# Two attention layers on one core: sums in the full array shape turned as whole tiles and added by DVE; layer-1 reciprocals spread one turn later, beside the maxima

## The chip, the cores and the metric

The kernel runs on one core of a Trainium2 chip. The metric is the time of one execution on the device, in microseconds (us). The engines are TensorE (PE in the profile; PEld is its weight load), VectorE (DVE), ScalarE (ACT), GpSimd (POOL) and SyncE (SP, which here only issues DMAs). All data are 32-bit floats.

## The reference

Two attention layers over images of 4 x 128 channels x 4096 positions (64 x 64). For each of the 4 images:

```
layer 0:  g, theta, phi = 1x1 projections of x to 64 channels
          f = theta^T phi                      (4096 x 4096)
          x = W (softmax(f) g) + b + x         (128 channels again)
layer 1:  q, k, v = 1x1 projections of x, 128 channels
          x = x + softmax(q^T k / sqrt(128)) v
```

The softmax runs over the 4096 keys of each query. For it a kernel needs, per query, the largest score, the exponentials of the scores less that maximum, and their sum.

## The kernel before, in words

The work is cut into 64 chunks, each of 512 queries of one image and one layer: 8 chunks per image and layer. The first 8 are layer 0 of image 0. Then layer-0 chunks of the next image alternate with layer-1 chunks of this one (chunks 8 to 55), and the last 8 are layer 1 of image 3. The list is `chunks`; chunk g is its g-th entry.

A chunk's keys are taken in 16 pieces p of 256 (two halves of 128, the partitions of a tile). Score tiles therefore have keys on partitions and the 512 queries along the free dimension, 128 x 2 x 512. The program is one long hand-written order: `slot(t)` writes the instructions of slot t, 16 slots to a turn, and the instructions of each engine run in the order in which the slots write them. In turn T the scores of chunk T are made; the later steps of the earlier chunks run beside them:

- `scores` (slot t, PE, lines 187 and 246) writes a score tile `ps` in PSUM. There are two of these tiles, so the scores of slot p wait until those of slot p-2 have been read.
- `copy` (ACT, L253) copies ps to SBUF as `s`; `maxima` (DVE, L260 and L262) takes the running maximum `mx` of ps. The maximum of a slot is the last reader of its ps.
- At the next turn's start `max_merge` (DVE, L265) folds the two halves of mx; at slot 1 `max_turn` (PE, L270) turns mx by four transposes into `pt`, `max_columns` (DVE, L275) takes the maximum along the free dimension, and `max_spread` (PE, L282) spreads it again over all partitions by four more transposes, as `o_mx`.
- `subtract` (DVE, L290) 18 slots after the scores, `exps` (ACT, L294) after 19, `sums` (POOL, L306, L308 and L311) right behind them: POOL adds the 16 exponential tiles of a chunk into `sum`, 128 partitions x 512 queries in the end. `values` (PE, lines 343 to 356) multiplies with the values 20 and 21 slots after the scores and gathers `acc` (and in one mode `hi`) in PSUM.
- `leave` (ACT L360, DVE L362) moves acc to SBUF as `y`, at slot 4, two turns after the scores.

What is left of a chunk is done by `finish()` in three steps, at slots that `out_slots(g)` gives:

- `sum_columns` and `invert`: sum still has one partial sum per partition. Matmuls with a column of ones as the moving operand add over the partitions, 128 queries at a time, into `pc` (128 x 4, queries on partitions, PE, L187); DVE takes the reciprocal `rc` (L373).
- `sum_spread` and `normalize`: four transposes spread rc over all partitions as `o_rc` (PE, L282), and DVE multiplies y by it (L381).
- `project_out` and `residual`: in layer 0 the projection W (PE, `po`), then y or po, the bias and x are added on DVE (L393 in layer 0, L396 in layer 1). In layer 1 the result goes out by DMA (L397), and the next x tile is loaded (L90).

`pt`, `pc`, `o_rc`, `po` and the query projection `pq` all use the one PSUM tile of the pool `ps_m`; each has to be read before the next is written.

The array of PE is used in three shapes. `mode(t)` names the one of a pair of slots by what runs in them: "row" (scores of layer 0 beside values of layer 1; 64 rows, two matmuls at once), "col" (layer 0 on either side; 64 columns, two at once), and "full" (layer 1 on both sides). `cut` splits a matmul into two halves of 64 columns in col mode. The transposes always use the whole array.

In the alternating stage a layer-1 chunk's three steps come at slots 7, 9 and 11 of the second turn after its own, which scores a layer-1 chunk too. Those of a layer-0 chunk would fall into a row-mode turn there and come at slots 1, 3 and 5 of the turn after, again one that scores a layer-1 chunk. So before the change all three steps of both kinds lie in turns with layer-1 scores. At slots above 5, `finish()` follows the maxima of the slot; at slots up to 5 it follows the values, and `max_spread` if there is one.

Of the kernel before, what the change touches and what calls it, by code (L numbers as in the profile page):

```python
# [10 lines left out]
F32 = mybir.dt.float32  # L11
AF = mybir.ActivationFunctionType
ALU = mybir.AluOpType
AX = mybir.AxisListType
# [3 lines left out]
def kernel(  # L18
# [39 lines left out]
    nc = tc.nc  # L58
    B, C, N = x.shape
    IC = thT.shape[1]  # L60
    P = 128
    NB = 512
    NCH = N // NB
    KT = NB // P
    NPR = N // (2 * P)
# [10 lines left out]
    w2 = ctx.enter_context(tc.tile_pool(name="w2", bufs=2))  # L76
# [4 lines left out]
    ps_m = ctx.enter_context(tc.tile_pool(name="ps_m", bufs=1, space=bass.MemoryType.PSUM))  # L81

    def const(name, shape):
        return cp.tile(shape, F32, tag=name, name=name)
# [10 lines left out]
    ident = const("ident", [P, P])  # L95
# [64 lines left out]
    chunks = [(0, 0, c) for c in range(NCH)]  # L160
# [5 lines left out]
    NG = len(chunks)  # L166
    begin = {ch: BT * g for g, ch in enumerate(chunks)}

    def layer_at(t, lag):
        g = (t - lag) // NPR  # L170
        return chunks[g][0] if 0 <= g < NG else None

    def mode(t):

        t -= t % 2
        ls, lv = layer_at(t, 0), layer_at(t, VL)
        if ls == 0 and lv == 1:
            return "row"
        return "col" if lv == 0 or ls == 0 else "full"

    now = ["full"]

    def cut(out, lhsT, rhs, start=True, stop=True):

        cols = [slice(0, IC), slice(IC, P)] if now[0] == "col" else [slice(0, P)]
        for c in cols:
            nc.tensor.matmul(out[c], lhsT=lhsT[:, c], rhs=rhs, start=start, stop=stop)  # L187
# [8 lines left out]
    SUM = {}  # L196
# [31 lines left out]
    def proj_q(g):  # L228
        layer, b, c = chunks[g]
        pq = ps_m.tile([P, NB], F32, tag="m", name=f"pq_{g}")  # L230
        cut(pq, weights[layer][0], X[b, c])
        q = w3.tile([P, NB], F32, tag="q", name=f"q_{g}")
        nc.scalar.activation(q, pq, AF.Identity, bias=weights[layer][1])
        Q[g] = q
# [29 lines left out]
    def max_merge(g):  # L264
        nc.vector.tensor_tensor(M[g][:, 0, :], M[g][:, 0, :], M[g][:, 1, :], ALU.max)  # L265

    def max_turn(g):
        pt = ps_m.tile([P, KT, P], F32, tag="m", name=f"pt_{g}")
        for i in range(KT):
            nc.tensor.transpose(pt[:, i, :], M[g][:, 0, ts(i, P)], ident)  # L270
        M[g] = pt

    def max_columns(g):
        mc = w2.tile([P, KT], F32, tag="mc", name=f"mc_{g}")
        nc.vector.reduce_max(mc, M[g], AX.X)  # L275
        M[g] = mc
# [8 lines left out]
    def max_spread(g):  # L285
        BC[g] = spread(ps_b, "b", f"mx_{g}", M.pop(g))
# [71 lines left out]
    def leave(g):  # L358
        y = w2.tile([P, NB], F32, tag="y", name=f"y_{g}")
        nc.scalar.copy(y, ACC.pop(g))  # L360
        if g in HI:
            nc.vector.tensor_tensor(y, HI.pop(g)[0], y, ALU.add)  # L362
        ACC[g] = y

    def sum_columns(g):
        pc = ps_m.tile([P, KT], F32, tag="m", name=f"pc_{g}")
        for i in range(KT):
            cut(pc[:, i : i + 1], SUM[g][:, 0, ts(i, P)], ones[:, 0:1])
        SUM[g] = pc

    def invert(g):
        rc = w2.tile([P, KT], F32, tag="rc", name=f"rc_{g}")
        nc.vector.reciprocal(rc, SUM[g])  # L373
        SUM[g] = rc

    def sum_spread(g):
        SUM[g] = spread(ps_m, "m", f"rc_{g}", SUM[g])

    def normalize(g):
        y = ACC[g]  # L380
        nc.vector.tensor_tensor(y, y, SUM.pop(g), ALU.mult)  # L381

    def project_out(g):
        if chunks[g][0] == 0:
            po = ps_m.tile([P, NB], F32, tag="m", name=f"po_{g}")
            cut(po, wo0, ACC[g])
            ACC[g] = po

    def residual(g):
        layer, b, c = chunks[g]  # L390
        if layer == 0:
            t = X[b, c]
            nc.vector.scalar_tensor_tensor(t, ACC.pop(g), bo0, t, ALU.add, ALU.add)  # L393
        else:
            t = X.pop((b, c))
            nc.vector.scalar_tensor_tensor(t, ACC.pop(g), bv1, t, ALU.add, ALU.add)  # L396
            nc.sync.dma_start(out=out[b, :, ts(c, NB)], in_=t)  # L397
            if loads:
                load(*loads.pop(0))

    def out_slots(g):

        t = (g + 2) * NPR
        if chunks[g][0] == 0 and mode(t + 8) == "row":
            return [t + NPR + q for q in (1, 3, 5)]
        return [t + q for q in (7, 9, 11)]

    def query_slot(g):
        t = (g - 1) * NPR + 13
        return t if mode(t) != "row" else (g - 2) * NPR + 15  # L410

    queries = {query_slot(g): g for g in range(1, NG)}
    cols, spreads, outs = ({out_slots(g)[k]: g for g in range(NG)} for k in range(3))

# [2 lines left out]
    def at(table, batch, *job):  # L419
        table.setdefault(batch, []).append(job)  # L420

    at(later, BT, small_products, 0, 0)
    for b in range(B):
        at0, at1 = begin[0, b, 0], begin[1, b, 0]
        for j in range(NCH):
            if b == 0:
                if j:
                    at(mid, j - 1, keys0, b, j)
                at(later, BT + 1 + j, values0, b, j)
            elif b == 1:  # L430
                at(mid, at0 - 7 + j, keys0, b, j)
                at(later, at0 + 2 + j, values0, b, j)
            else:
                at(mid if j < NCH - 2 else later, at0 - 6 + j, keys0, b, j)
                at(later, at0 - 6 + j, values0, b, j)
            ready = out_slots(chunks.index((0, b, j)))[2] // 2 + 1
            at(later, max(ready, at1 - (7 if b == B - 1 else 9) + j), keys1, b, j)
            at(later, max(ready, at1 + 2 + j), values1, b, j)

    def of(t, lag):  # L440

        g, p = divmod(t - lag, NPR)
        return (g, p) if 0 <= g < NG else None

    def run(fn, gp):
        if gp is not None:
            fn(*gp)

    def slot(t):
        turn, p = divmod(t, NPR)  # L450
        m = turn - 1 if 0 <= turn - 1 < NG else None
        now[0] = mode(t)
        f = turn - 2 if 0 <= turn - 2 < NG else None
        if p == 0 and m is not None:
            max_merge(m)
        if p == 4 and f is not None:
            leave(f)
        run(scores, of(t, 0))
        run(copy, of(t, 0))
        run(exps, of(t, EL))  # L460
        run(sums, of(t, EL))
        run(subtract, of(t, SL))
        if p == 1 and m is not None:
            max_turn(m)
            max_columns(m)
        run(maxima, of(t, 0))
        run(own_sums, of(t, EL + 1))

        def finish():
            if t in cols:  # L470
                sum_columns(cols[t])
                invert(cols[t])
            if t in spreads:
                sum_spread(spreads[t])
                normalize(spreads[t])
            if t in outs:
                project_out(outs[t])
                residual(outs[t])
            if t in queries:
                proj_q(queries[t])  # L480

        if p > 5:
            finish()
        if p % 2 == 0:
            for fn, b, j in mid.get(t // 2, []):
                fn(b, j)
        else:
            run(values, of(t, VL + 1))
            run(values, of(t, VL))
            if p == 1 and m is not None:  # L490
                max_spread(m)
            if p <= 5:
                finish()
            for fn, b, j in later.get(t // 2, []):
                fn(b, j)
# [41 lines left out]
```

## Time and profile before

| | |
|---|---|
| median of 3 runs | 3079.7 us (3072.96 to 3080.42) |
| the profiled execution | 3076.04 us |
| its span | 3074.3 us |
| granted PE clock over the span | 0.998 |
| busy: PE, DVE, POOL, ACT | 3019.3, 2532.6, 2383.8, 2096.9 us |
| pc matmuls, full shape / in 64 columns | 264 / 496 records, 31.5 / 18.4 us |
| pt, o_mx, o_rc transposes | 256 records each, 40.3, 40.1, 40.5 us |
| L275 reduction along the free dimension | x64, mean 0.684 us |
| L381 normalize / L396 residual of layer 1 | x64, mean 0.682 us / x32, mean 0.774 us |

A row of the groups or of a timeline names the line, the engine, the operation, and the tiles "out<-in" with shapes; a timeline line begins with start and duration in us, and several instructions of a kind that follow each other are merged with their count. In brackets stands the idle time of the engine just before, and what ended it. A matmul of 32-bit floats appears as two records, a transpose as one. Matmuls overlap in the pipeline, so a group's duration runs into the next group; the distance from start to start is the time that it takes from the engine.

### The profile page before, as it was taken

To read this page: it belongs to the slowest core of one execution; us is meant where nothing else is said; L and a number is where in the kernel's file an instruction comes from. 1 tells how busy PE (TensorE), PEld (TensorE's weight loads), DVE (VectorE), ACT (ScalarE), POOL (GpSimd) and SP (SyncE) were. 2 spreads that over 40 slices of the span, in tenths; PEclk is the share of its full clock that TensorE was granted. 3 is DMA by queue.
4 is the path that set the end of the run, shared out by engine and by line. 5 is a ranking of instruction groups with operands and counts; after the bars stand their busy time and mean duration, and the time that the engine had idled before them with its cause. 6 is when DMAs were issued, how large, how long until landed. Compare 5 with 4: busy or idle time off the path is not lost.

```text
span 3074.3 us, 35878 instructions
## 1 busy us (share of the span) xinstructions
PE 3019.3 (98%) x13484; PEld 1243.5 (40%) x13484; DVE 2532.6 (82%) x2337; ACT 2096.9 (68%) x2306; POOL 2383.8 (78%) x1025
## 2 busy tenths in 40 slices
PE   8999999999999999999999999999999999999998
PEld 3222343344443444433344444444333444444444
DVE  6999878888888788888888877888888886766677
ACT  6888867666667676776666776667766676555554
POOL 3999878777888677887878877788878776666667
PEclk9999999999999999999999999999999999999999
DMA  2000000000000000000000000000000000000000
GB/s 67 1 1 1 1 1 8 8 8 4 4 8 8 8 8 1 8 8 8 7 6 2 8 4 4 4 1 4 4 4 4 4 0 4 4 4 7 4 4 11
DMA packets 11534, 19.47 MB, mean 6 GB/s; under 512 B 2656, under 2 KB 3168, under 8 KB 11360
## 3 DMA queue, kind: packets, MB, share of 16 engines
q1 hardware_dynamic: 10896, 17.14, 1.7%
q8 instruction: 106, 1.74, 0.2%
q14 instruction: 68, 0.56, 0.1%
q10 hardware_dynamic: 464, 0.03, 0.0%
HBM read 8.79 MB, written 8.39 MB: 6 GB/s over the span
## 4 chain that ended last, share of the span: by engine, by line
PE 88%; DVE 6%; issue 3%; ACT 3%; POOL 1%; ACTq 0%; DVEq 0%; POOLq 0%
PE ps L187 29%; PE acc L351 15%; PE acc L356 12%; PE ps L246 11%; PE acc L343 11%; DVE mx L262 5%; PE pq L187 2%; ACT s L253 2%; PE pv L187 1%; PE pc L187 1%; PE pt L270 1%; PE o_mx L282 1%; DVE s L290 1%; PE o_rc L282 1%; PE po L187 1%
## 5 line engine op out<-in xcount | busy, mean ns | idle before, releaser
L308 POOL TENSOR_TENSOR sum<-sum,s 128x1024 f32<-128x1024 f32 x891 | 2150.6, 2414 | 494.5 <-ACT s L294 450.9
L253 ACT COPY s<-ps 128x1024 f32<-128x1024 f32 x1024 | 1032.2, 1008 | 853.7 <-PE ps L187 560.4
L262 DVE TENSOR_TENSOR mx<-ps,mx 128x1024 f32<-128x1024 f32 x896 | 1093.9, 1221 | 417.6 <-ACT s L253 417.0
L290 DVE TENSOR_TENSOR s<-s,o_mx 128x1024 f32<-128x1024 f32 x1024 | 1233.2, 1210 | 15.1 <-PE o_mx L282 13.3
L294 ACT ACTIVATE s<-s 128x1024 f32<-128x1024 f32 x1024 | 1090.0, 1065 | 16.5 <-DVE s L290 16.1
L187 PE MATMUL ps<-q,k 128*64 128x512 f32 (+1 forms) x3232 | 929.5, 594 | 2.8 <-ACT k L217 2.8
L246 PE MATMUL ps<-q,k 64*128 64x512 f32 x2048 | 519.3, 613 | 25.4 <-DVE mx L262 24.1
L187 PEld LDWEIGHTS ps<-q,k 128*64 128x64 f32 (+1 forms) x3232 | 325.5, 151 | 506.3 <-issue 445.0
L343 PE MATMUL acc<-s,v 128*64 128x512 f32 x2048 | 497.8, 601 | 8.7 <-ACT s L294 8.7
L352 PE MATMUL hi<-s,v 64*128 64x512 f32 x1104 | 496.0, 589 | 0.0
L351 PE MATMUL acc<-s,v 64*128 64x512 f32 x1104 | 496.0, 589 | 0.0
L356 PE MATMUL acc<-s,v 128*128 128x512 f32 x944 | 424.8, 593 | 0.8 <-ACT y L360 0.7
L351 PEld LDWEIGHTS acc<-s,v 64*128 64x128 f32 x1104 | 205.9, 187 | 260.7 <-issue 202.7
L246 PEld LDWEIGHTS ps<-q,k 64*128 64x128 f32 x2048 | 179.6, 186 | 299.9 <-DVE mx L262 149.1
L306 POOL TENSOR_TENSOR sum<-s,s 128x1024 f32<-128x1024 f32 x64 | 152.1, 2376 | 180.8 <-ACT s L294 180.5
L356 PEld LDWEIGHTS acc<-s,v 128*128 128x128 f32 x944 | 175.3, 190 | 203.3 <-issue 187.4
L343 PEld LDWEIGHTS acc<-s,v 128*64 128x64 f32 x2048 | 131.0, 136 | 279.7 <-issue 157.0
L352 PEld LDWEIGHTS hi<-s,v 64*128 64x128 f32 x1104 | 205.9, 187 | 0.0
L260 DVE TENSOR_TENSOR mx<-ps,s 128x1024 f32<-128x1024 f32 x64 | 78.0, 1218 | 22.5 <-ACT s L253 18.9
L265 DVE TENSOR_TENSOR mx<-mx 128x512 f32<-128x512 f32 x64 | 90.4, 1413 | 2.2
L311 POOL TENSOR_TENSOR sum<-sum 128x512 f32<-128x512 f32 x63 | 80.3, 1275 | 4.9
L187 PE MATMUL pq<-x,wq 128*64 128x512 f32 (+1 forms) x240 | 66.6, 598 | 0.0
(49 smaller groups left out, 846.0 us busy)
## 6 DMA issues: line engine op xcount, KB each, us to landing
x<-in_x_dram SPq DMA_DIRECT2D x32, 256.0 KB, 3.3
out_dram<-x SPq DMA_DIRECT2D x32, 256.0 KB, 2.0
wq<-in_theta_wT_dram SPq DMA_DIRECT2D x2, 32.0 KB, 2.9
wo<-in_W_wT_dram SPq DMA_DIRECT2D x2, 32.0 KB, 4.7
wk<-in_Wk_dram SPq DMA_DIRECT2D x1, 64.0 KB, 2.9
wv<-in_Wv_dram SPq DMA_DIRECT2D x1, 64.0 KB, 2.3
wq<-in_Wq_dram SPq DMA_DIRECT2D x1, 64.0 KB, 1.8
wk<-in_phi_wT_dram ACTq DMA_DIRECT2D x1, 32.0 KB, 3.2
```

Of the source, the lines that this page charges most:

```text
L187: nc.tensor.matmul(out[c], lhsT=lhsT[:, c], rhs=rhs, start=start, stop=stop)
L246: nc.tensor.matmul(ps[:, h, :], lhsT=K[0, b, j][rows, r, :], rhs=q[rows, :], start=True, stop=True)
L253: nc.scalar.copy(s, PS[g, p])
L262: nc.vector.tensor_tensor(M[g], ps, M[g], ALU.max)
L290: nc.vector.tensor_tensor(s, s, BC[g].unsqueeze(1).to_broadcast([P, 2, NB]), ALU.subtract)
L294: nc.scalar.activation(s, s, AF.Exp, scale=scales[chunks[g][0]])
L306: nc.gpsimd.tensor_tensor(SUM[g], S[g, 0], s, ALU.add)
L308: nc.gpsimd.tensor_tensor(SUM[g], SUM[g], s, ALU.add)
L343: nc.tensor.matmul(ACC[g][h * IC : (h + 1) * IC, :], lhsT=v, rhs=s[:, h, :], start=first, stop=last)
L351: nc.tensor.matmul(ACC[g], lhsT=v[lo], rhs=s[lo, h, :], start=first, stop=last)
L352: nc.tensor.matmul(hi, lhsT=v[up], rhs=s[up, h, :], start=(p == p0 and h == 0), stop=(p == p1 and h == 1))
L356: nc.tensor.matmul(ACC[g], lhsT=v, rhs=s[:, h, :], start=first, stop=last)
```

## The change

`sum_columns` has a second form. In full mode it turns the four 128 x 128 pieces of sum by transposes, as `max_turn` does with the maxima, into a `pc` of 128 x 4 x 128, and DVE adds along the free dimension (`reduce_sum`) into `sc`, 128 x 4 in SBUF; `invert` takes its reciprocal from there. In the other modes it is as before.

`out_slots` now gives four slots, with normalize apart from the spread. For most chunks these are the old ones. For a layer-1 chunk whose finishing turn runs in col mode, the reciprocals stay at slot 7; the spread goes to slot 1 of the next turn, where it follows `max_spread`, and normalize and residual go to slot 6 of that next turn, between the maxima of slots 6 and 7. That next turn scores a layer-0 chunk, but for the last such chunk.

```diff
--- before.py
+++ after.py
@@ -363,6 +363,15 @@
         ACC[g] = y
 
     def sum_columns(g):
+        if now[0] == "full":
+
+            pc = ps_m.tile([P, KT, P], F32, tag="m", name=f"pc_{g}")
+            for i in range(KT):
+                nc.tensor.transpose(pc[:, i, :], SUM[g][:, 0, ts(i, P)], ident)
+            sc = w2.tile([P, KT], F32, tag="sc", name=f"sc_{g}")
+            nc.vector.reduce_sum(sc, pc, AX.X)
+            SUM[g] = sc
+            return
         pc = ps_m.tile([P, KT], F32, tag="m", name=f"pc_{g}")
         for i in range(KT):
             cut(pc[:, i : i + 1], SUM[g][:, 0, ts(i, P)], ones[:, 0:1])
@@ -400,17 +409,20 @@
 
     def out_slots(g):
 
+
         t = (g + 2) * NPR
         if chunks[g][0] == 0 and mode(t + 8) == "row":
-            return [t + NPR + q for q in (1, 3, 5)]
-        return [t + q for q in (7, 9, 11)]
+            return [t + NPR + q for q in (1, 3, 3, 5)]
+        if chunks[g][0] == 1 and mode(t + 8) == "col":
+            return [t + 7, t + NPR + 1, t + NPR + 6, t + NPR + 6]
+        return [t + q for q in (7, 9, 9, 11)]
 
     def query_slot(g):
         t = (g - 1) * NPR + 13
         return t if mode(t) != "row" else (g - 2) * NPR + 15
 
     queries = {query_slot(g): g for g in range(1, NG)}
-    cols, spreads, outs = ({out_slots(g)[k]: g for g in range(NG)} for k in range(3))
+    cols, spreads, norms, outs = ({out_slots(g)[k]: g for g in range(NG)} for k in range(4))
 
 
 
@@ -433,7 +445,7 @@
             else:
                 at(mid if j < NCH - 2 else later, at0 - 6 + j, keys0, b, j)
                 at(later, at0 - 6 + j, values0, b, j)
-            ready = out_slots(chunks.index((0, b, j)))[2] // 2 + 1
+            ready = out_slots(chunks.index((0, b, j)))[3] // 2 + 1
             at(later, max(ready, at1 - (7 if b == B - 1 else 9) + j), keys1, b, j)
             at(later, max(ready, at1 + 2 + j), values1, b, j)
 
@@ -472,7 +484,8 @@
                 invert(cols[t])
             if t in spreads:
                 sum_spread(spreads[t])
-                normalize(spreads[t])
+            if t in norms:
+                normalize(norms[t])
             if t in outs:
                 project_out(outs[t])
                 residual(outs[t])
```

## Prediction

> **What bounds the kernel now.** I read the page's busy times and chain first, then the PE timeline of one steady pair of turns (a turn is the 16 slots of one chunk), then DVE and POOL in the same stretch.
>
> ```profile
> PE 3019.3 (98%) x13484; PEld 1243.5 (40%) x13484; DVE 2532.6 (82%) x2337; ACT 2096.9 (68%) x2306; POOL 2383.8 (78%) x1025
> ...
> PE 88%; DVE 6%; issue 3%; ACT 3%; POOL 1%; ACTq 0%; DVEq 0%; POOLq 0%
> ```
>
> TensorE has work nearly always and 88% of the chain is its own, so an operation taken off PE is worth its start-to-start time, except where PE waits for someone. Busy time hides where that is. A turn that scores a layer-1 chunk runs on the PE timeline from 2044.66 to 2095.62, 50.96 us; a turn that scores a layer-0 chunk from 2003.64 to 2044.66, 41.02 us. DVE's fixed work per turn (16 maxima, 16 subtractions, each starting 1.13 us after the last) is 36.2 us in both. So the layer-0 turns are where DVE is close to the bound, and the change moves work into them.
>
> The layer-1 turn on PE:
>
> ```profile
> 2048.20 0.60 PE L270 MATMUL pt<-ident,mx 128*128 128x128 f32 x4
> 2048.63 3.60 PE L356 MATMUL acc<-s,v 128*128 128x512 f32 x8
> 2052.07 0.60 PE L282 MATMUL o_mx<-ident,mc 128*128 128x128 f32 x4
> 2052.51 0.95 PE L187 MATMUL pc<-ones,sum 128*128 128x1 f32 x8
> 2053.32 3.68 PE L187 MATMUL ps<-q,k 128*128 128x512 f32 x8
> ...
> 2072.47 3.60 PE L187 MATMUL ps<-q,k 128*64 128x512 f32 x16
> 2076.01 0.65 PE L282 MATMUL o_rc<-ident,rc 128*128 128x128 f32 x4
> 2076.59 1.94 PE L343 MATMUL acc<-s,v 128*64 128x512 f32 x8
> 2078.36 3.60 PE L187 MATMUL ps<-q,k 128*64 128x512 f32 x16
> 2081.79 1.89 PE L343 MATMUL acc<-s,v 128*64 128x512 f32 x8
> 2083.51 3.60 PE L187 MATMUL ps<-q,k 128*64 128x512 f32 x16
> ```
>
> Read the distances between starts, not the durations. Four transposes take 0.43 (pt) or 0.44 (o_mx); the eight passes of pc take 0.81. The lone o_rc at slot 9 stretches its surroundings: 2072.47 to 2078.36 is 5.89, where the next pair without it, 2078.36 to 2083.51, is 5.15. It costs 0.74. No line here has an idle bracket, so PE sets this turn.
>
> The layer-0 turn, PE, then DVE and POOL:
>
> ```profile
> 2014.42 1.13 PE L246 MATMUL ps<-q,k 64*128 64x512 f32 x4 [0.43 <-DVE mx L262]
> ...
> 2023.96 1.88 PE L246 MATMUL ps<-q,k 64*128 64x512 f32 x8
> ```
>
> ```profile
> 2020.98 1.22 DVE L262 TENSOR_TENSOR mx<-ps,mx 128x1024 f32<-128x1024 f32 x1 [0.97 <-ACT s L253]
> ...
> 2022.05 4.83 POOL L308 TENSOR_TENSOR sum<-sum,s 128x1024 f32<-128x1024 f32 x2 [1.11 <-ACT s L294]
> 2022.12 1.21 DVE L290 TENSOR_TENSOR s<-s,o_mx 128x1024 f32<-128x1024 f32 x1
> ...
> 2023.25 1.22 DVE L262 TENSOR_TENSOR mx<-ps,mx 128x1024 f32<-128x1024 f32 x1
> ```
>
> These DVE lines are the maximum of slot 6, a subtraction, and the maximum of slot 7, which ends at 2024.47 and frees the score buffer that slot 9 needs. Slot 9's scores are the second half of the group at 2023.96, so they start at 2024.82. The margin is 0.35. In the three slots before, it is already gone: at 2014.42 PE waits for such a maximum.
>
> **The savings.** Sums turned in full mode: the order of the changed kernel has 33 of them: 23 at slot 1 of the layer-1 turns, 9 in the all-layer-1 stage, one in the tail. Each swaps pc (0.81) for four transposes (0.44), 0.37. On 32 of them PE is the bound: 11.8 us. The added DVE reduction is the twin of max_columns (0.68, 33 times, 22 us of DVE); it stands ahead of a subtraction in a DVE queue that waits 2.63 us for pc there, and the following maximum waits 1.63 for ACT anyway. I cost it at nothing; without that cover it would cost up to 0.68 each. The reciprocal reads 128x4 as before.
>
> The spread o_rc leaves slot 9 of 23 layer-1 turns: 23 x 0.74 = 17.0 us. Together 28.8.
>
> **The costs.** o_rc goes behind o_mx at slot 1 of the next turn, in whole-array mode already paid for: 0.44. There PE's lead is not free: the next scores start the copy, the maximum and the scores of slot 5 that wait for it, so all shifts by 0.44. 23 x 0.44 = 10.1.
>
> Normalize and residual go from slots 9 and 11 of the layer-1 turn to slot 6 of the next turn, between the maxima of slots 6 and 7. In 22 cases that is a layer-0 turn; the 23rd falls into the full stage, where the same margin is 3.87 us. What is queued behind them on DVE is a subtraction and the maximum of slot 7; PE waits for that. Two instructions by their rows: normalize 0.68; the residual waits for it, and DVE rows that wait for their predecessor (L381 then L396 in the tail) start 0.72 after it; the next starts 0.66 after a residual of 0.74. So 0.72 + 0.66 = 1.38 late.
>
> But the residual (L396) reads two SBUF tiles, y and x. What such an instruction does while POOL is adding is seen in two places:
>
> ```profile
> 3046.05 6.00 POOL L308 TENSOR_TENSOR sum<-sum,s 128x1024 f32<-128x1024 f32 x2
> ...
> 3048.10 1.72 DVE L396 SCALAR_TENSOR_TENSOR x<-y,bv,x 128x512 f32<-128x512 f32 x1
> ```
>
> ```profile
> 2134.63 4.79 POOL L308 TENSOR_TENSOR sum<-sum,s 128x1024 f32<-128x1024 f32 x2 [0.34 <-ACT s L294]
> ...
> 2137.08 2.89 DVE L265 TENSOR_TENSOR mx<-mx 128x512 f32<-128x512 f32 x1
> 2139.89 1.21 DVE L290 TENSOR_TENSOR s<-s,o_mx 128x1024 f32<-128x1024 f32 x1
> ```
>
> The first is the slowest of 32 residuals (the others take 0.74): POOL's add ended 1.17 us after it was issued, and it took that plus 0.55. The second is the merge of maxima, 0.69 in 43 turns and 2.9 in 21: there it was issued just behind the start of an add (here the second of the two, at 2137.07) and sat out its 2.35. All 30 other residuals under POOL work were issued within 0.05 us of an add's end, which is why the row looks harmless. Normalize reads one PSUM operand and takes 0.68 whatever POOL does.
>
> At its new place the residual is issued at 2020.98 + 1.14 + 0.72 = 2022.84. POOL's add started at 2022.05 (released by ACT, so tied to the same slot) and ends at 2024.42. The offset, 0.79 into the add, is the same to 0.01 in all 22 layer-0 turns. So the residual ends at 2024.42 + 0.55 = 2024.97; the subtraction starts at 2024.90, the maximum of slot 7 at 2026.03, ending 2027.25. PE's slot 9 starts 0.06 later, as at 2014.42, at 2027.31 instead of 2024.82: 2.49, and 0.10 more, since those scores took 0.96 to the next line after that stall instead of 0.86. **A new wait of 2.59 us, 22 times: 57.0 us.** The next pair absorbs the lag: DVE's maximum of slot 9 would end at 2031.78, before PE's slot 11 at 2032.56. Bounds: from below -0.35 + 0.06 + 1.38 + 0.10 = 1.19 (no wait for POOL), from above 2.59 + 2.45 (a second add goes first). I take 2.59, the reading of the 22 rows above.
>
> [...]
>
> [...]
>
> The tail: the last chunk's column sums stand alone. Transposes there take 1.22 to their reader (as o_rc at 3068.03 to 3069.25), then 0.71 for the reduction, against pc's 1.12: +0.8.
>
> **Sum.** -28.8 + 10.1 + 57.0 + 0.8 = +39.1. The profiled execution took 3076.04 (span 3074.3 and 1.7 around it), 3.7 under the median of three, 3079.7. Forecast 3115, about 1.3% slower. About 0.3%, 9 us, is what a measurement of this kernel can tell from no change.
>
> **Rivals.**
> 1. The residual doesn't sit out the add (the slow rows being something else). The wait is 1.19: 26.2 instead of 57.0, +8.3, **3084**. For it: 31 quick residuals. Against: their place at the ends of adds.
> 2. The buffer margin isn't what stops PE, because DVE makes up the lag before slot 9. Then only savings, o_rc and tail remain: -17.9, **3058**, faster. It decides once the pair's lateness stays under 0.29. Against: 2014.42 waits for exactly this release.
> [...]
>
> Chances: forecast 0.74 (own range 3102 to 3127: 0.3 us a turn and the spread of the times), rival 1 0.14, rival 2 0.06, rival 3 0.03, else 0.03. The range runs from rival 1, 3082, to 3127. Rival 1 is split around the 9 us bound. Faster 0.06, same 0.11, slower 0.83.
>
> **What would show it.** Layer-0 turns of about 44 us instead of 41.02; residual rows near 2.1 us; PE waiting some 2.5 us for the maximum at slot 9; layer-1 turns near 49.85; pc at 0.44 to its successor. Residuals at 0.74 in layer-0 turns make it rival 1; no wait at slot 9 makes it rival 2. I am wrong as well if the shorter layer-1 turn shifts POOL against DVE, or if the reduction at slot 1 delays a maximum.

## The result, and the profile after

The changed kernel takes 3147.26 us (median of 6 runs, 3144.21 to 3147.71) against 3075.99 us before (median of 6): a ratio of 1.0229, 95% interval 1.0218 to 1.0239. The forecast was 3115 us, and 3147 lies above its range, which ended at 3127. The profiled execution took 3147.71 us with a span of 3145.9, so 71.6 us more span than before.

The page of the changed kernel (the busy times and the chain, which the prediction shows for the kernel before), and its group of layer-0 scores:

```profile
PE 3035.9 (97%) x13352; PEld 1240.3 (39%) x13352; DVE 2569.9 (82%) x2370; ACT 2102.8 (67%) x2306; POOL 2386.9 (76%) x1025
...
PE 82%; DVE 10%; ACT 3%; issue 3%; POOL 2%; DMA 0%; POOLq 0%; ACTq 0%; DVEq 0%
...
L246 PE MATMUL ps<-q,k 64*128 64x512 f32 x2048 | 531.9, 622 | 75.7 <-DVE mx L262 74.5
```

PE's share of the chain falls from 88 to 82%, DVE's rises from 6 to 10. PE waits 74.5 us for maxima in front of layer-0 scores. The same group before:

```profile
L246 PE MATMUL ps<-q,k 64*128 64x512 f32 x2048 | 519.3, 613 | 25.4 <-DVE mx L262 24.1
```

PE's busy time grows by 17 us although it has 132 records fewer: its instructions themselves became slower.

The layer-1 turn after, on PE:

```profile
2108.57 0.60 PE L282 MATMUL o_mx<-ident,mc 128*128 128x128 f32 x4
2109.01 0.60 PE L370 MATMUL pc<-ident,sum 128*128 128x128 f32 x4
2109.44 3.60 PE L187 MATMUL ps<-q,k 128*128 128x512 f32 x8
```

Four transposes take 0.43 where the eight passes took 0.81. By the starts of the turns' first scores, each of the 23 layer-1 turns from turn 11 on is 1.19 us shorter (50.96 to 49.77 in a steady one).

The layer-0 turn after, first DVE, then PE:

```profile
2073.22 1.23 DVE L262 TENSOR_TENSOR mx<-ps,mx 128x1024 f32<-128x1024 f32 x1 [0.97 <-ACT s L253]
2074.36 0.68 DVE L390 TENSOR_TENSOR y<-y,o_rc 128x512 f32<-128x512 f32 x1
2075.07 2.13 DVE L405 SCALAR_TENSOR_TENSOR x<-y,bv,x 128x512 f32<-128x512 f32 x1
2077.12 1.21 DVE L290 TENSOR_TENSOR s<-s,o_mx 128x1024 f32<-128x1024 f32 x1
2078.26 1.21 DVE L262 TENSOR_TENSOR mx<-ps,mx 128x1024 f32<-128x1024 f32 x1
```

```profile
2076.20 1.02 PE L246 MATMUL ps<-q,k 64*128 64x512 f32 x4
2079.52 1.17 PE L246 MATMUL ps<-q,k 64*128 64x512 f32 x4 [2.30 <-DVE mx L262]
2080.48 1.05 PE L351 MATMUL acc<-s,v 64*128 64x512 f32 x1
...
2081.33 1.05 PE L351 MATMUL acc<-s,v 64*128 64x512 f32 x1
...
2082.19 1.05 PE L351 MATMUL acc<-s,v 64*128 64x512 f32 x1
...
2083.04 1.02 PE L351 MATMUL acc<-s,v 64*128 64x512 f32 x1
...
2083.89 0.59 PE L351 MATMUL acc<-s,v 64*128 64x512 f32 x1
...
2084.33 0.59 PE L351 MATMUL acc<-s,v 64*128 64x512 f32 x1
```

The residual takes 2.13 us; the maximum behind it is late, and PE waits 2.30 us for it at slot 9. Then comes what the prediction had not: the four matmuls after the wait start 0.85 apart, twice the usual 0.43, and take up to 1.05 us instead of 0.59. The granted clock says why. The table of stretches of the same kernel, whose columns are the stretch, its length, the busy time and instructions of PE, PEld, DVE, ACT and POOL, the granted PE clock, the DMA share and GB/s:

```profile
2077.07:2080.48 3.41, 1.11 (x6) 0.49 (x6) 3.41 (x4) 2.07 (x2) 3.27 (x2) 1.00 0.20 77
2080.48:2083.89 3.41, 3.41 (x10) 1.36 (x8) 3.41 (x4) 1.97 (x2) 2.44 (x2) 0.50 0.00 0
2083.89:2087.31 3.42, 3.42 (x18) 1.55 (x16) 1.23 (x2) 0.57 (x1) 1.38 (x1) 1.00 0.00 0
```

PE worked 1.11 of 3.41 us, and for the next 3.41 us it got half its clock. That loses half of 3.41, 1.70 us, after the wait is over. It happened in 20 of the 22 layer-0 turns with a moved residual. Those turns are 4.7 us longer than before (41.02 to 45.71); turns 24 and 40, without it, 3.0.

So the 71.6 us come to this, from the turns' starts: 23 layer-1 turns at -1.19, -27.4; 22 layer-0 turns at +3.00, +66.0; 20 stretches of half clock at 1.70, +34.0; turn 12 once more +1.8 (a late merge of maxima, see the last section); turn 56 +1.6; turns 57 to 62 at -0.45, -2.7; the rest, head and tail, -1.7.

### The profile page after: what moved, and what is told of

Read it like the earlier page. It is cut to its first block, busy times and chain, and to the rows that moved or that the text cites. A ratio compares the mean times of both kernels' runs of the same rounds, so it can differ in the third digit from the quotient of the medians.

```text
span 3145.9 us, 35605 instructions
## 1 busy us (share of the span) xinstructions
PE 3035.9 (97%) x13352; PEld 1240.3 (39%) x13352; DVE 2569.9 (82%) x2370; ACT 2102.8 (67%) x2306; POOL 2386.9 (76%) x1025
## 4 chain that ended last, share of the span: by engine, by line
PE 82%; DVE 10%; ACT 3%; issue 3%; POOL 2%; DMA 0%; POOLq 0%; ACTq 0%; DVEq 0%
PE ps L187 28%; PE acc L351 13%; PE acc L356 12%; PE acc L343 11%; PE ps L246 10%; DVE mx L262 6%; ACT s L253 2%; DVE s L290 2%; POOL sum L308 2%; DVE x L405 2%; PE pq L187 2%; PE pv L187 1%; PE o_mx L282 1%; PE pt L270 1%; PE o_rc L282 1%
## 5 line engine op out<-in xcount | busy, mean ns | idle before, releaser
L262 DVE TENSOR_TENSOR mx<-ps,mx 128x1024 f32<-128x1024 f32 x896 | 1092.7, 1220 | 439.1 <-ACT s L253 438.5
L246 PE MATMUL ps<-q,k 64*128 64x512 f32 x2048 | 531.9, 622 | 75.7 <-DVE mx L262 74.5
L351 PE MATMUL acc<-s,v 64*128 64x512 f32 x1104 | 523.3, 616 | 0.0
L352 PE MATMUL hi<-s,v 64*128 64x512 f32 x1104 | 523.2, 616 | 0.0
L351 PEld LDWEIGHTS acc<-s,v 64*128 64x128 f32 x1104 | 217.1, 197 | 282.4 <-issue 227.8
L352 PEld LDWEIGHTS hi<-s,v 64*128 64x128 f32 x1104 | 217.1, 197 | 0.0
L260 DVE TENSOR_TENSOR mx<-ps,s 128x1024 f32<-128x1024 f32 x64 | 78.1, 1220 | 23.5 <-ACT s L253 19.0
L265 DVE TENSOR_TENSOR mx<-mx 128x512 f32<-128x512 f32 x64 | 72.8, 1138 | 2.2
```

The source lines that it names most:

```text
L246: nc.tensor.matmul(ps[:, h, :], lhsT=K[0, b, j][rows, r, :], rhs=q[rows, :], start=True, stop=True)
L262: nc.vector.tensor_tensor(M[g], ps, M[g], ALU.max)
L351: nc.tensor.matmul(ACC[g], lhsT=v[lo], rhs=s[lo, h, :], start=first, stop=last)
L352: nc.tensor.matmul(hi, lhsT=v[up], rhs=s[up, h, :], start=(p == p0 and h == 0), stop=(p == p1 and h == 1))
```

## The experiments

The theory after the result: the moved residual sits out POOL's add, which makes PE wait 2.3 us at slot 9, and a PE that idles for 2.30 us of a 3.41 us stretch, as in the rows above, gets half its clock in the next. The rivals: the DVE work itself is too much there; or the clock falls for some other reason, such as the new transposes. Each kernel is timed against the kernel before on the same chip.

### e1: a residual with one SBUF operand

The edit, shortened (`moved` names the 23 moved chunks; it is defined beside this):

```diff
     def normalize(g):
         y = ACC[g]
+        if moved(g):      # layer 1, finishing turn in col mode
+            o = SUM.pop(g)
+            nc.vector.tensor_tensor(o, y, o, ALU.mult)
+            ACC[g] = o
+            return
```

> The change, but normalize writes its product over o_rc in PSUM, so that the moved residual reads one PSUM and one SBUF operand. Theory (the residual sits out POOL's add; PE then waits 2.3 us for the maximum of slot 7, and the granted clock halves for 3.4 us after so long a wait): residual 0.74 us, PE's wait at slot 9 about 1.0 us, no stretch of half clock in the alternating stage, layer-0 turns near 42.7 us, 3081 us. Rival (two more DVE instructions in a tight turn are the cause, whatever they read): the wait stays 2.3 us and the time near 3147. Rival (the loss of clock comes from the new transposes or from the moved spread): the half-clock stretches stay, 3115.

Measured: 3087.32 us, ratio 1.0038 (1.0024 to 1.0051). DVE and PE around slot 9:

```profile
2121.45 0.69 DVE L395 TENSOR_TENSOR o_rc<-y,o_rc 128x512 f32<-128x512 f32 x1
2122.17 0.75 DVE L413 SCALAR_TENSOR_TENSOR x<-o_rc,bv,x 128x512 f32<-128x512 f32 x1
2122.84 1.21 DVE L290 TENSOR_TENSOR s<-s,o_mx 128x1024 f32<-128x1024 f32 x1
2123.97 1.22 DVE L262 TENSOR_TENSOR mx<-ps,mx 128x1024 f32<-128x1024 f32 x1
```

```profile
2125.24 1.13 PE L246 MATMUL ps<-q,k 64*128 64x512 f32 x4 [0.93 <-DVE mx L262]
```

The same two instructions at the same place, with the product now in PSUM instead of SBUF: the residual takes 0.75 us, the wait falls from 2.30 to 0.93, the clock stays whole in all 22 turns, and they are 42.65 us long (+1.63). 60 of the 71 us are gone. The work itself costs the 1.2 us a turn that the prediction's lower bound gave; the rest hangs on the pair of SBUF operands. The 6 us above the expectation of 3081 are turn 56 (+4.0, where o_rc now keeps the one ps_m tile through the residual and the next chunk's column sums wait for it, with one stretch of half clock) and one late merge of maxima in turn 44 (+1.9).

### e2: work for PE during the wait

Shortened: the condition is written out in the kernel, and `zeros` is a new tile of zeros.

```diff
+        if p == 9 and ...:     # the 22 layer-0 turns with a moved residual
+            for _ in range(3):
+                nc.tensor.matmul(ACC[m], lhsT=zeros, rhs=Q[turn], start=False, stop=False)
         run(scores, of(t, 0))
```

> The change, with three matmuls (zero weights, added into acc, 0.86 us each) in front of the scores of slot 9 in the 22 layer-0 turns, so that PE works while it waits. Theory (the clock drops because PE idles): no half-clock stretch in the alternating stage, layer-0 turns near 44.1 us instead of 45.7, 3113 to 3116 us. Rival (the clock drops for another reason): the stretches stay, and the time is 3147 or a little more.

Measured: 3125.13 us, ratio 1.0158 (1.0144 to 1.0171); 22 us less than the change although each of these turns does three matmuls more.

```profile
2153.24 1.02 PE L248 MATMUL ps<-q,k 64*128 64x512 f32 x4
2154.20 2.84 PE L474 MATMUL acc<-q,zeros 128*128 128x512 f32 x6
2156.97 1.13 PE L248 MATMUL ps<-q,k 64*128 64x512 f32 x4
```

No stretch of half clock is left in the alternating stage; the turns are 44.43 us, +3.41, where the change had +4.69. The residuals are still 2.1 us. The filling takes 2.77 from start to start, a little longer than the wait, and two merges were late (3.8 us, turns 22 and 28); these put it above the expectation. It settles that PE's idling brings the half clock, not the transposes, the moved spread or the residual.

### e3 and e4: the two parts alone

e3 is the kernel before with the new branch of `sum_columns` only; e4 is the change without it:

```diff
# e4
     def sum_columns(g):
-        if now[0] == "full":
-            pc = ps_m.tile([P, KT, P], F32, tag="m", name=f"pc_{g}")
...
-            SUM[g] = sc
-            return
```

> The kernel before with the turned sums alone, old slots. Theory: 32 sums on PE's path get 0.37 to 0.45 us shorter, the tail 0.8 longer: 3062 to 3065 us. Rival (the reduction on DVE delays a maximum or a subtraction): 3076 or more, with waits of PE for DVE in the layer-1 turns.

Measured: 3070.49 us, ratio 0.9977 (0.9968 to 0.9986); the profiled span is 5.4 us below before's. The 23 layer-1 turns are each 0.46 shorter and the full turns 0.45; those 32 make 14.6 us. 5.7 us of that came off in this execution by late merges in turns 8, 38 and 50, 1.88 each, and 2.2 by a later start of turn 8; in the profiled executions of the changed kernels that start lies between 3.5 us before and 2.5 us behind that of before. No wait of PE for the reduction shows, so the first part is what it set out to be, a small gain. The expectation was 5.5 to 8.5 us too low; it had left the late merges out.

> The change without the turned sums: the old pc matmuls in all modes, the new slots. Theory: the whole loss is in the slots: 12 to 14 us above the change, 3160 us, with the same 2.3 us waits and half-clock stretches. Rival (the transposes of the sums have a part in the loss of clock): nearer to 3147 or below, fewer stretches.

Measured: 3155.01 us, ratio 1.0261 (1.0247 to 1.0275). The whole loss is in the slots: layer-1 turns -0.73, layer-0 turns +3.00, or +4.7 with a stretch of half clock. The median is 5 us under the expectation of 3160; the profiled execution, 3164.01, was the slowest of four (the others 3153.63 to 3155.20), with 2.7 us more than the change ahead of turn 8 and 3.4 more from turn 63's start on. There are 19 stretches of half clock this time, and others escape: turns 16, 34 and 52, while 24 and 40 are hit. The wait was the same in all of them, 2.29 to 2.30 us. What differs is where it lies against stretches of 3.413 us that run on their own and not with the program. In the change's trace each of the 20 half-clock stretches of the layer-0 turns is 3.413 us long, and they start whole multiples of that apart (17 of the 19 distances are 28 times it, 95.57 us, the other two 60 times). In two steady pairs of turns the wait ends at 2079.52 and at 2175.01, 95.49 apart, but the half clock begins at 2080.48 and at 2176.05, 95.57 apart. In e4:

```profile
1887.68:1891.09 3.41, 1.42 (x8) 0.72 (x10) 3.41 (x4) 2.06 (x3) 3.26 (x2) 1.00 0.20 77
1891.09:1894.50 3.41, 3.41 (x12) 1.38 (x10) 3.41 (x4) 2.48 (x3) 2.47 (x2) 0.50 0.00 0
```

```profile
713.49:716.90 3.41, 1.48 (x8) 0.39 (x4) 3.41 (x3) 2.07 (x3) 3.33 (x2) 1.00 0.20 77
716.90:720.32 3.42, 3.06 (x14) 1.46 (x16) 3.42 (x4) 2.09 (x3) 2.61 (x2) 1.00 0.25 81
```

In turn 40 (the first pair) and turn 16 (the second) part of the 2.30 us wait fell into the neighbouring stretch. PE worked 1.42 of 3.41 in the one and 1.48 in the other, so it was idle for 1.99 and 1.93, and the clock halved after the one and not after the other. In turns 8 to 62 of the ten kernels every stretch with 1.99 us idle or more was followed by half clock (62 of them), and none with 1.94 or less.

Outside these turns it is not so. In the second turn of the kernel before, a stretch with 1.81 us idle was followed by half clock:

```profile
46.70:50.12 3.42, 1.61 (x20) 0.65 (x16) 3.32 (x3) 3.06 (x5) 0.00 (x0) 1.00 0.00 0
50.12:53.53 3.41, 3.19 (x8) 1.04 (x10) 3.41 (x4) 2.17 (x4) 2.22 (x1) 0.50 0.00 0
```

PE's work there includes 16 records of short matmuls (128x64). So idle time as this profile gives it does not alone say which stretch is followed by half clock, and what else does stays open.

### e8a and e8b: the wait made longer without POOL

e1 with one or two multiplications by 1.0 on the PSUM tile ahead of the residual (they change no value):

```diff
             nc.vector.tensor_tensor(o, y, o, ALU.mult)
+            if chunks[g + 3][0] == 0:
+                for _ in range(1):      # e8b: 2
+                    nc.vector.tensor_scalar_mul(o, o, 1.0)
```

> e1 with one more multiplication by 1.0 in place on the PSUM tile (0.7 us) ahead of the residual in the 22 layer-0 turns; no operand pair in SBUF. Theory: PE's wait at slot 9 grows from 1.0 to 1.7 us, which stays below what halved the clock (up to 1.75 us idle in a 3.413 us stretch did not, 2.01 did): no half-clock stretches, or few; layer-0 turns 43.4 us; 3103. Rival (the clock follows something of POOL or of the residual, not PE's idle time): no half clock at all in e8a and e8b.

> e1 with two such multiplications. Theory: the wait is 2.4 us without POOL having a part, and the clock halves in most of the 22 turns as in the change: layer-0 turns 44.1 us without and 45.8 with half clock, 3145 to 3155. Rival (the clock follows POOL or the residual, not PE's idle time): no half clock, 3119.

Measured, one run each: e8a 3106.49 us, e8b 3152.27. In e8a the wait is 1.66 us, none of the 22 turns has a stretch of half clock, and they are +2.36, but for 14 and 28, where a late merge makes it +4.25; the time is 3.5 us above the expectation of 3103, and these two merges cost 3.8. One wait of e8a, which lies in one stretch as a whole, and the stretch behind it:

```profile
2141.87 1.13 PE L246 MATMUL ps<-q,k 64*128 64x512 f32 x4 [1.66 <-DVE mx L262]
```

```profile
2139.42:2142.84 3.42, 1.76 (x10) 0.50 (x8) 3.42 (x4) 1.97 (x2) 3.00 (x3) 1.00 0.20 77
2142.84:2146.25 3.41, 3.41 (x18) 1.54 (x16) 3.41 (x4) 1.97 (x2) 2.99 (x2) 1.00 0.00 0
```

In e8b the wait is 2.39, as long as in the change but with a residual of 0.75:

```profile
2077.84 1.43 DVE L398 TENSOR_SCALAR o_rc<-o_rc 128x512 f32<-128x512 f32 x2
...
2079.30 0.75 DVE L416 SCALAR_TENSOR_TENSOR x<-o_rc,bv,x 128x512 f32<-128x512 f32 x1
...
2082.37 1.70 PE L246 MATMUL ps<-q,k 64*128 64x512 f32 x4 [2.39 <-DVE mx L262]
```

20 of the 22 turns have their stretch of half clock and are +4.79, two are +3.10. So 0.73 us more wait costs 0.73 us a turn, and the next 0.73 costs 2.43 in most. The order of causes is shown: POOL's add, the late maximum, PE's wait, the clock; and the last step needs only the wait.

### e5 and e6: the same work in DVE's gaps

```diff
# e6; e5 also has e1's product in PSUM
-            return [t + 7, t + NPR + 1, t + NPR + 6, t + NPR + 6]
+            q = (7, 9) if chunks[g + 3][0] == 0 else (6, 6)
+            return [t + 7, t + NPR + 1, t + NPR + q[0], t + NPR + q[1]]
```

> The change, but normalize of the 22 moved chunks (product in PSUM, as in e1) comes behind the maximum of slot 7 and the residual behind that of slot 9, so that each falls into one of the 0.54 us gaps that DVE has ahead of an even slot. Theory: no wait of PE at slots 9 or 11 beyond that of before, layer-0 turns 0.5 us longer (o_rc alone), layer-1 turns 1.19 shorter, no half clock: 3058 to 3062 us, faster than both. Rival (any DVE work in these turns is paid in full): 22 x 1.2 us more, 3086.

> As e5, but with the product in SBUF, so the residual at slot 9 reads two SBUF operands again. Theory: it is issued within 0.1 us of the end of one of POOL's adds (by the rows of before: DVE at 2029.5, add boundary at 2029.6); if ahead of the next add it costs 0.74 us and the time is that of e5, if behind it 2.9 us, a wait of PE at slot 11 near 2 us and some half clock: 3058 to 3062 or 3105 to 3145. Rival (the slow residual is not POOL's doing): 3058 to 3062 with residuals that are not tied to the adds' ends.

Measured: e5 3061.61 us, ratio 0.9945 (0.9931 to 0.9959); e6 3059.69 us, ratio 0.9938 (0.9924 to 0.9952). Both beat both kernels. The layer-0 turns are 41.45 us, o_rc's 0.44 and nothing else. In e6:

```profile
2107.24 5.31 POOL L308 TENSOR_TENSOR sum<-sum,s 128x1024 f32<-128x1024 f32 x2 [0.32 <-ACT s L294]
...
2107.31 1.21 DVE L290 TENSOR_TENSOR s<-s,o_mx 128x1024 f32<-128x1024 f32 x1
2108.44 1.22 DVE L262 TENSOR_TENSOR mx<-ps,mx 128x1024 f32<-128x1024 f32 x1
2109.57 0.74 DVE L405 SCALAR_TENSOR_TENSOR x<-y,bv,x 128x512 f32<-128x512 f32 x1
2110.23 1.21 DVE L290 TENSOR_TENSOR s<-s,o_mx 128x1024 f32<-128x1024 f32 x1
```

Here the residual has its two SBUF operands again and takes 0.74, for it is issued just before POOL's first add ends; it is then POOL that waits, and its two adds take 5.31 instead of 4.83. The margin is 0.03 us in the trace, so this rests on a coincidence of phases, held in all 22 turns; e5 doesn't depend on it. e5's 2 us more fit turn 56, which is +4.0 as in e1, and +1.6 in e6.

## Why the prediction was wrong, point by point

- **The savings** were right and a little small: a layer-1 turn lost 1.19 against 0.37 + 0.74 = 1.11; a turned sum saved 0.45, not 0.37; the starts of the lines above give 0.38 for the swap itself, and where the other 0.07 comes from is open.
- **The reduction at no cost**: right (e3).
- **o_rc at 0.44**: right (e5, e6).
- **The residual that sits out POOL's add**: right in mechanism and size. 2.12 us at the median for a forecast 2.13 (2024.97 less 2022.84), PE's slot 9 late by 2.46 for 2.49, layer-0 turns +3.00 for 0.44 + 2.59 where the clock stayed whole. e1 shows the mechanism; rival 1 (3084) is what e1 built, and what the change did not do. Rival 2 did not come, and neither did the upper bound's second add ahead of the residual: PE waited 2.30 us at slot 9.
- **The step that failed** is the price of that wait: "A new wait of 2.59 us, 22 times: 57.0 us". I priced what follows a wait by 0.10, from the 0.43 us wait at slot 5. After a wait of 2.3 us PE worked at half clock for 3.41 us, 1.70 us lost in 20 of 22 turns: 34.0 us that stood in no term and in no bound of the range. With them the sum is 39.1 + 34.0 = 73.1 for a measured 71.6. The hint was there in the same trace and I read past it: before has three stretches at half clock (at its start, at its end, and at 50.1 us, the rows under e4, behind two waits of PE, 0.90 and 1.13 us), and the mean granted clock of 0.998 is not 1.
- **Two readings of the layer-0 turn** were off without bearing on the sum. A turn has 15 maxima, not 16 (960 rows of L260 and L262 for 64 chunks), so DVE's fixed work is 35.0 us and not 36.2. And of the slots ahead of slot 9 only slot 5 waits for a maximum.
- **The tail** cost 0.3 instead of 0.8 (1.40 from the first transpose to the reciprocal, against 1.12).
- **Turn 56** was costed at o_rc alone, +0.44, and came to +1.6: ps_m is held until normalize at slot 6, and the column sums of the next chunk, at slot 7, wait 1.39 us for it.

What the layer-0 turns show of the clock is this: PE idle for 1.99 us of one 3.41 us stretch (e4) was followed by half clock in the next, PE idle for 1.93 (e4) or 1.66 (e8a) was not.

## What to carry to other kernels

A wait of the bound engine is not priced by its length alone: look at what share of a 3.41 us stretch it empties. Here 1.66 us (e8a, no half clock) and 2.30 us (the change, half clock in 20 of 22 turns) differed in kind. Before a DVE instruction with two SBUF operands is moved, lay its new issue time over POOL's instructions; its usual duration says nothing about another phase (the residual took 0.74 or 0.75 us in 31 of 32 cases before, and 2.12 at the median of the moved ones). And work put between two maxima is paid or free by half a slot: behind the odd maximum it fell into a gap (e5, layer-0 turns of 41.45 us), behind the even one it stopped PE (e1, the same work, 42.65).

## What the runs showed of the hardware

- The merge of maxima (L265, two SBUF operands) is issued in nearly every steady turn within 0.02 us of the start of a POOL add, and which comes first differs from turn to turn. Behind the add it takes 2.9 us instead of 0.69 (21 and 43 of the 64 before). At the start of a layer-1 turn that costs nothing (before, 50.97 us to the next merge from 2137.08, where it took 2.89, and from 2045.10, where it took 0.69); at the start of a layer-0 turn it costs 1.8 to 1.9 us: turn 12 of the change, turns 8, 38 and 50 of e3, 22 and 28 of e2, 44 of e1, 14 and 28 of e8a, none in before, e4, e5, e6 and e8b. It may move the time of one and the same kernel from run to run; e3's runs lie between 3064 and 3076 us, but one execution of each kernel was profiled, so how much of that spread the merges make is not shown.
- Filling a wait with useless matmuls can pay: e2 does 66 matmuls more than the change and is 22 us faster.
